# Another account for the split of the maxima, and order rules for seven attention steps

## The chip, the cores and the metric

The kernel runs on one core of a Trainium2 chip. The metric is the device time of one execution in microseconds. The core has a matrix engine (TensorE, PE in the profile), a vector engine (VectorE, DVE), a scalar engine (ScalarE, ACT), GpSimd (POOL) and a queue that issues transfers (SyncE, SP). They run side by side, each through its own list of instructions in order, and wait for each other by semaphores.

## The reference

A transformer block with a modulation by a condition, on 8 sequences of 1024 tokens with 512 features, 16 heads of 32, all in f32:

```python
mod = jax.nn.silu(condition) @ Wada + bada
sh_a, sc_a, gt_a, sh_m, sc_m, gt_m = jnp.split(mod, 6, axis=1)
xn = _layernorm(x, g1, be1)
xm = xn * (1.0 + sc_a[:, None, :]) + sh_a[:, None, :]
x = x + gt_a[:, None, :] * _attention(xm, Wqkv, Wproj, bproj)
xn = _layernorm(x, g2, be2)
xm = xn * (1.0 + sc_m[:, None, :]) + sh_m[:, None, :]
h = jax.nn.gelu(xm @ W1 + b1, approximate=False)
x = x + gt_m[:, None, :] * (h @ W2 + b2)
```

`_attention` is causal: scores of q and k times 32^-0.5, masked above the diagonal, softmax over the keys, times v, and the projection.

## The kernel before

The tokens are worked in 16 blocks of 512; blocks 2b and 2b+1 are the halves of sequence b. All linear layers (q, k, v, the projection, the two layers of the MLP) are products in the manner of Strassen: seven block products in place of eight, with sums of weights kept in DRAM and sums of activations (`t_a`, `t_m`, `qT`, `hT`) made on VectorE or GpSimd. Their matmuls (L233) go to three banks of PSUM and are taken out by ScalarE (L217) or VectorE (L222).

Attention goes through the groups (n, g): block n and four of the heads, g = 0 to 3. For a group, TensorE computes scores with the queries on the partitions (`sc`, L1828). VectorE adds the mask where the diagonal is (L1842) and reduces them to a maximum for each query and head (`mx`, L1845); in an odd block the two halves are combined (L1859). `split_maxima` writes each maximum as three bf16 numbers into `mcols` with four small instructions (L1864 to L1867), on GpSimd or VectorE. TensorE transposes them into a bank (L1883), ScalarE copies them out as `mrow` (L1889). Then TensorE computes the transposed logits less the maxima (`st`, L1909 and L1921), ScalarE takes the exponential (`pT`, L1934), GpSimd blanks the masked triangle (L1939) and adds the weights for the sums (L2047), and TensorE multiplies with v (`po`, L1962) and sums the weights (L1983). `sc` and `st` share one region of PSUM, called "st" in the code. So each must wait until the one before has been reduced or exponentiated.

Attention alone doesn't fill TensorE. The products of the linear layers are a second stream, cut in pieces of four matmuls, and the program is written down by a planner that runs as the kernel is built. It keeps an account of when each engine would be free (`now`) and each result there (`written`, `left`); every instruction that it emits adds a fixed number of ns by `note`. Before each step of attention, `step_aside` emits linear products until the account says that the step's operands are ready. Nothing of this account is seen by the chip: it decides only in which order the instructions stand on each engine, and, in `sooner` and `either`, which engine gets an elementwise instruction.

Two numbers of that planner can be set for each group (n, g), in the table `MANNER`; groups that don't stand in it have (1000, 0):

```python
margin[0], leaning[0] = MANNER.get((n, g), (1000, 0))
```

The first, `margin`, is the lead in ns that VectorE must have over GpSimd in the account for `either` to give it an instruction. The second, `leaning`, is by how many ns `step_aside` lets a step of attention go ahead of, or after, linear products: ahead of its operands' readiness when the linear stream is behind its due share, and otherwise as soon as its own wait is no longer than that of the linear stream by more than so much.

Blocks 3 to 13 have their normalised rows turned by transfers before the MLP: SP writes the rows to DRAM (`turned_m<-xm_m`, L852) and reads four columns back (`xm_m<-turned_m`, L858); VectorE or ScalarE modulates each column (L918, L924), and sums of them are made (L932, L934, L187, L190) for the products that read `xm_m` and `t_m`. Weights come through a ring of nine tiles (`w`, L391 and L393), loaded in order as a tile is released by its last product.

Of the kernel before, what the change touches and what calls it, by code (L numbers as in the profile page):

```python
# [22 lines left out]
def kernel(  # L23
# [81 lines left out]
    def due(reads=(), writes=()):  # L105
        t = 0.0
        for k in reads:
            t = max(t, written.get(k, 0.0))
        for k in writes:
            t = max(t, left.get(k, 0.0))  # L110
        return t

    def give_way(start, end):

        if not any(start <= a < end for a, *_ in pool_spans):
            return
        for i, (a, b, reads, writes) in enumerate(pool_spans):
            if a < start:
                continue
            if a >= end:  # L120
                break
            later = end, end + b - a
            pool_spans[i] = *later, reads, writes
            for of, keys in ((left, reads), (written, writes)):
                for k in keys:
                    if of.get(k) == b + SYNC:
                        of[k] = later[1] + SYNC
            end = later[1]
        now["POOL"] = max(now["POOL"], end)

    def note(engine, ns, reads=(), writes=(), port=False):
        start = max(now[engine], due(reads, writes))
        if port:
            start = max([start] + [b for a, b, *_ in pool_spans if a <= start < b])
            give_way(start, start + ns - FREE)
        elif engine == "POOL":
            start = max([start] + [b for a, b in port_spans if a <= start < b])
        end = start + ns
        now[engine] = end
        if port:  # L140
            port_spans.append((start, end - FREE))
            del port_spans[:-16]
        elif engine == "POOL":
            pool_spans.append((start, end, reads, writes))
            del pool_spans[:-16]
        for k in reads:
            left[k] = max(left.get(k, 0.0), end + SYNC)
        for k in writes:
            written[k] = end + SYNC
        return end  # L150
# [134 lines left out]
    for w in range(1, NB):  # L285
        n = w - 1
# [26 lines left out]
    n = NB - 1  # L313
# [145 lines left out]
    for some in row_sets:  # L459
        count = sum(n for _, n in some)  # L460
        rows = tmp.tile([P, TB], F32, tag="y", name=f"rows_{first_row}")[:count, :P]
# [1246 lines left out]


    TRIANGLE = [[0], [1, 3], [2]]  # L1710
    MANNER = {(0, 1): (1000, 300), (0, 3): (1000, 300), (1, 3): (-1000, 0), (2, 0): (-1000, 0), (2, 1): (2500, 0), (3, 1): (0, 0), (4, 0): (1000, 300), (6, 0): (1000, 300), (8, 0): (1000, 300), (10, 0): (1000, 300), (12, 1): (2500, 0), (14, 3): (0, 0), (3, 3): (2500, 300)}
    groups = [(n, g) for n in range(NB) for g in range(NC)]

    def score_units(n, g):
# [54 lines left out]
    def scores(n, g, parts):  # L1769

        h = blocks[n][1]
        for gg in {part[4]: None for part in parts}:
            if (n, gg) not in maxima:
                maxima[n, gg] = small.tile([P, 2, NTT, HPG], F32, tag="mx", name=f"mx_{n}_{gg}")
        reads = [("qT", n), ("kT", n - h + parts[0][1])]
        if (
            linear_wait() > 3000
            and not any(live)
            and wait_of((reads, ["st"])) > wait_of((reads, [BANK])) + 1000
        ):  # L1780
            scores_by_heads(n, g, parts, reads)
        else:
            scores_at_once(n, g, parts, reads)
        if units[unit_at[0] + 1 :] == [] or units[unit_at[0] + 1][:2] != (n, g):
            split_maxima(n, g, h)
# [64 lines left out]
    def split_maxima(n, g, h):  # L1850


        mx = maxima.pop((n, g))
        m = mx[:, 0, :, :]
        split = mcols.rearrange("p t (j c) -> p t j c", c=hd)
        high, middle, low = (split[:, :, :, i] for i in range(3))
        rest = small.tile([P, NTT, HPG], F32, tag="rest", name=f"rest_{n}_{g}")
        if h:
            nc.vector.tensor_tensor(m, m, mx[:, 1, :, :], ALU.max)  # L1859
            note("DVE", 180, [("mx", n, g)], [("mx", n, g)], port=True)  # L1860
        ready = due([("mx", n, g)])
        on_pool = max(now["POOL"], ready) + 1000 < max(now["DVE"], ready) + 2200
        engine = nc.gpsimd if on_pool else nc.vector
        engine.tensor_copy(high, m)  # L1864
        engine.tensor_tensor(rest, m, high, ALU.subtract)
        engine.tensor_copy(middle, rest)
        engine.tensor_tensor(low, rest, middle, ALU.subtract)  # L1867
        for _ in range(4):
            if on_pool:
                note("POOL", 250, [("mx", n, g)], [("rows", n, g)])  # L1870
            else:
                note("DVE", 180, [("mx", n, g)], [("rows", n, g)], port=True)
        rows_due.append((n, g))
# [176 lines left out]
    def attend():  # L2050
        previous = None
        for n in range(NB):
# [23 lines left out]
            for g, k, n_slots, upto in slots:  # L2076
                margin[0], leaning[0] = MANNER.get((n, g), (1000, 0))
                if (n, g) == groups[-1]:
# [153 lines left out]
```

## Time and profile before

| | |
|---|---|
| time, median of 3 runs | 3445.95 us |
| the runs | 3452.72, 3445.95, 3444.2 us |
| the profiled execution: its own time | 3444.65 us |
| its span, first to last instruction | 3442.9 us |
| TensorE, matmuls busy | 3414.4 us (99%) |
| VectorE busy | 2070.1 us (60%) |
| GpSimd busy | 1920.2 us (56%) |
| ScalarE busy | 1283.6 us (37%) |
| transfers, read and written over the span | 140 GB/s |
| granted TensorE clock | 1.000 |

Busy time is the time in which an instruction of the engine runs. TensorE's share leaves 28.5 us of the span; the other engines' idle time costs nothing as long as TensorE doesn't wait for them. A row of the waits names the waiting engine and line, what it waited for, and the total, the number and the longest of these waits in us. In rows of the timeline stand start, duration, engine, line, what is written and read, and in square brackets the idle time of the engine before it and what ended that.

### The profile page before, as it was taken

Reading aid. Unit: us, or ns where it says so; the run is one execution under the profiler, and the core shown is the slowest. Engines: PE = TensorE matmul, PEld = TensorE weight load, DVE = VectorE, ACT = ScalarE, POOL = GpSimd, SP = SyncE. Lnnn points to the kernel's source line nnn. Section 1 sums busy time; section 2 is a strip of 40 time slices with the busy share of each in tenths; the row PEclk is TensorE's granted clock in tenths of the full one; section 3 lists DMA queues with packets and bytes.
Section 4 is the critical chain, followed back from the end, with each engine's and each line's share of the span. In section 5 each row is a group of like instructions: output and inputs, shape, how many; then the busy total and the mean of one; then the engine's idle time right before and its main releaser. Section 6 shows DMA issues by size and latency. Waiting matters only on the chain.

```text
span 3442.9 us, 122860 instructions
## 1 busy us (share of the span) xinstructions
PE 3414.4 (99%) x55594; PEld 1772.7 (51%) x55594; DVE 2070.1 (60%) x2317; ACT 1283.6 (37%) x1418; POOL 1920.2 (56%) x2088
## 2 busy tenths in 40 slices
PE   8999999999999999999999999999999999999999
PEld 5544554455544555455554455454554545545555
DVE  6765666647566475664657546575566756556463
ACT  2345244333243333434344342432524335142431
POOL 3576755756267572675626755377553765447430
PEclk9999999999999999999999999999999999999999
DMA  6842434345544455444544445444464454533444
GB/s 231 279 129 85 119 116 137 102 120 156 170 136 130 129 159 157 133 139 130 167 142 133 136 137 171 136 133 141 129 186 129 126 149 148 167 109 103 121 142 137
DMA packets 380532, 490.69 MB, mean 143 GB/s; under 512 B 28487, under 2 KB 236511, under 8 KB 380010
## 3 DMA queue, kind: packets, MB, share of 16 engines
q1 hardware_dynamic: 379814, 482.54, 46.8%
q8 instruction: 438, 7.18, 0.9%
q14 instruction: 84, 0.69, 0.1%
q10 hardware_dynamic: 196, 0.28, 0.0%
HBM read 429.18 MB, written 53.53 MB: 140 GB/s over the span
## 4 chain that ended last, share of the span: by engine, by line
PE 92%; ACT 3%; DVE 3%; DMA 1%; issue 1%; POOL 1%; SPq 0%; DVEq 0%; ACTq 0%; POOLq 0%
PE bank L233 64%; PE sc L1828 9%; PE po L1962 7%; PE st L1921 7%; PE st L1909 3%; PE bank L1983 2%; DVE mx L1845 1%; ACT pT L1934 1%; ACT hT L1331 1%; PE bank L1883 0%; DMA xm_m<-turned_m 0%; DVE sc L1842 0%; ACT L1331 0%; PE bank L909 0%; ACT L170 0%
## 5 line engine op out<-in xcount | busy, mean ns | idle before, releaser
L2047 POOL TENSOR_TENSOR pT<-pT,pT 128x256 f32<-128x256 f32 (+3 forms) x1254 | 1221.5, 1010 | 173.9 <-ACT pT L1934 136.2
L1934 ACT ACTIVATE pT<-st 128x2048 f32<-128x2048 f32 x288 | 541.2, 1879 | 974.6 <-PE st L1921 884.0
L233 PE MATMUL bank<-w,hT 128*32 128x256 f32 x14336 | 812.9, 380 | 0.0
L1845 DVE TENSOR_REDUCE mx<-sc 128x4 f32<-128x2048 f32 (+3 forms) x384 | 665.6, 1754 | 210.5 <-PE sc L1828 204.3
L233 PEld LDWEIGHTS bank<-w,hT 128*32 128x32 f32 x14336 | 454.3, 110 | 357.0 <-issue 72.3
L233 PE MATMUL bank<-xm_m,w 128*32 128x256 f32 x8192 | 500.2, 380 | 0.8 <-ACT p_u L217 0.8
L233 PE MATMUL bank<-t_m,w 128*32 128x256 f32 x6144 | 381.2, 380 | 0.2
L233 PEld LDWEIGHTS bank<-xm_m,w 128*32 128x32 f32 x8192 | 255.0, 110 | 229.2 <-issue 65.4
L1939 POOL TENSOR_SCALAR_AFFINE_SELECT pT<-pT 128x512 f32<-128x512 f32 x256 | 172.2, 691 | 351.4 <-ACT pT L1934 349.9
L1828 PE MATMUL sc<-kT,qT 32*128 32x512 f32 (+3 forms) x3072 | 329.1, 520 | 1.3 <-DVE mx L1845 1.1
L1842 DVE TENSOR_TENSOR sc<-sc,mask 128x1024 f32<-128x1024 f32 (+1 forms) x160 | 162.8, 1017 | 245.3 <-PE sc L1828 181.5
L1962 PE MATMUL po<-pT,v 128*32 128x512 f32 (+3 forms) x3072 | 304.5, 491 | 0.0
L1921 PE MATMUL st<-qT,kT 32*128 32x512 f32 (+3 forms) x3072 | 300.0, 486 | 0.0
L233 PEld LDWEIGHTS bank<-t_m,w 128*32 128x32 f32 x6144 | 189.8, 110 | 174.7 <-issue 45.6
L233 PE MATMUL bank<-xm_a,w 128*32 128x256 f32 x3968 | 238.8, 380 | 1.7 <-ACT xm_a L924 1.1
L190 POOL TENSOR_TENSOR qT<-top,rec 128x512 f32<-128x512 f32 x58 | 75.4, 1300 | 284.2 <-ACT rec L2001 280.6
L1828 PEld LDWEIGHTS sc<-kT,qT 32*128 32x128 f32 x3072 | 129.4, 183 | 159.6 <-issue 59.2
L222 DVE TENSOR_TENSOR hT<-bank,u_u 128x512 f32<-128x512 f32 x192 | 129.5, 685 | 122.3 <-PE bank L233 119.4
L233 PE MATMUL bank<-w,qT 128*32 128x256 f32 (+1 forms) x3008 | 187.7, 389 | 0.0
L233 PE MATMUL bank<-t_a,w 128*32 128x256 f32 x2944 | 178.8, 380 | 0.5 <-DVE qT L222 0.5
L233 PEld LDWEIGHTS bank<-xm_a,w 128*32 128x32 f32 x3968 | 126.4, 110 | 100.6 <-issue 18.6
L1331 ACT ACTIVATE hT<-hT,cols 128x512 f32<-128x512 f32 x256 | 164.0, 711 | 17.8 <-DVE hT L222 17.1
(251 smaller groups left out, 3393.9 us busy)
## 6 DMA issues: line engine op xcount, KB each, us to landing
w<-in_L_cond_W_dram SPq DMA_DIRECT2D x384, 256.0 KB
w<-kept_up_S SPq DMA_DIRECT2D x256, 256.0 KB
w<-kept_down_S SPq DMA_DIRECT2D x256, 256.0 KB
w<-kept_qkv_S SPq DMA_DIRECT2D x180, 256.0 KB
w<-in_L_cond_Wqkv_dram SPq DMA_DIRECT2D x147, 256.0 KB
hat<-in_x_dram SPq DMA_DIRECT2D x64, 256.0 KB
xr<-in_x_dram SPq DMA_DIRECT2D x64, 256.0 KB
out_dram<-xr SPq DMA_DIRECT2D x64, 256.0 KB
```

The lines of the kernel that those rows point to most:

```text
L222: nc.vector.tensor_tensor(out, src, other, op)
L233: nc.tensor.matmul(ps[r], columns, rhs, start=start, stop=stop, skip_group_check=True)
L1331: nc.scalar.activation(hT[:, i, :], hT[:, i, :], AF.Gelu, bias=cols[:, O_B1 + f : O_B1 + f + 1])
L1828: nc.tensor.matmul(sc[:, j, c0 : c0 + w], qTs[n][r, gg, ts(qt, P)], keys_of(n, kh)[r, gg, :w], start=True, stop=True, skip_group_check=True,)
L1842: nc.vector.tensor_tensor(place, place, shape_of.to_broadcast(place.shape), ALU.add)
L1845: nc.vector.tensor_reduce(maxima[n, gg][:, kh, qt, :], sc[:, :, c0 : c0 + w], axis=AX.X, op=ALU.max)
L1909: nc.tensor.matmul(st[:, j, c0 : c0 + w], minus_ones[r, :], row[r, TB - w :], start=(c0 == 0), stop=False, skip_group_check=True,)
L1921: nc.tensor.matmul(st[:, j, c0 : c0 + w], kT[r, gg, ts(k % NTT, P)], qT[r, gg, TB - w :], start=False, stop=True, skip_group_check=True,)
L1934: nc.scalar.activation(pT[:, :, :used], st[:, :, :used], AF.Exp, scale=scale)
L1939: nc.gpsimd.affine_select(diagonal, diagonal, pattern=[[0, HPG], [1, P]], compare_op=ALU.is_ge, fill=0.0, base=0, channel_multiplier=-1,)
L1962: nc.tensor.matmul(po[r, TB - w :], v[:, k % NTT, g * P + j * hd : g * P + (j + 1) * hd], pT[:, j, c0 : c0 + w], start=(k == 0), stop=last ...
L2047: nc.gpsimd.tensor_tensor(into, into, pT[:, j, c0 : c0 + w], ALU.add)
```

## The change

One number of the account and seven entries of the table:

```diff
-    MANNER = {(0, 1): (1000, 300), (0, 3): (1000, 300), ..., (3, 3): (2500, 300)}
+    MANNER = {(0, 1): (1000, 300), (0, 3): (1000, 600), ..., (3, 3): (2500, 300), (10, 3): (-1000, 0), (0, 2): (2500, 300), (4, 2): (2500, 0), (2, 3): (0, 0), (6, 1): (1000, 300), (12, 2): (2500, 0)}
...
         for _ in range(4):
             if on_pool:
-                note("POOL", 250, [("mx", n, g)], [("rows", n, g)])
+                note("POOL", 335, [("mx", n, g)], [("rows", n, g)])
```

Four notes stand for the four instructions of a split on GpSimd, so the account of a split goes from 1000 to 1340 ns. The entry of (0, 3) goes from (1000, 300) to (1000, 600); six groups that had (1000, 0) get entries of their own. What is computed stays. The instructions on TensorE are the same in number and kind; elementwise instructions move between VectorE, ScalarE and GpSimd.

Three places show how the order moves. The names have block and group in them (`sc_9_0_1_0`: scores of block 9, group 0, query tile 1, key half 0; `xm_m7`: block 7's modulated input of the MLP); a last number counts buffers. The first place is TensorE at the transposition of the second group's maxima (block 0, group 1), the rows of before and then those of now:

```order
L1921 MATMUL st_0_0_1_958<-qT_0_399,kT_0_304 128x384 x4
L1921 MATMUL st_0_0_1_958<-qT_0_399,kT_0_304 128x128 x4
L1883 LDWEIGHTS mcols_162
L1883 MATMUL bank_2_97<-ident_b_170,mcols_162 32x128
...
L1962 MATMUL po_0_0_1003<-pT_0_0_0_868,v_0_640 32x512 x4
L233 MATMUL bank_1_96<-t_a1_608,w_16_604 32x256 x8
```

```order
L1921 MATMUL st_0_0_1_958<-qT_0_399,kT_0_304 128x384 x4
L1921 MATMUL st_0_0_1_958<-qT_0_399,kT_0_304 128x128 x4
L233 MATMUL bank_1_96<-t_a1_608,w_16_604 32x256 x8
L1883 LDWEIGHTS mcols_162
L1883 MATMUL bank_2_97<-ident_b_170,mcols_162 32x128
...
L1962 MATMUL po_0_0_1021<-pT_0_0_0_868,v_0_640 32x512 x4
```

Eight matmuls of a linear product that stood behind the transposition now stand ahead of it.

The second place is TensorE at the first scores of block 9, among the first products of block 7's MLP, before and now:

```order
L233 MATMUL bank_2_97<-t_a9_19618,w_657_20563 32x256 x16
L1828 MATMUL sc_9_0_0_0_20758<-kT_8_18068,qT_9_20462 128x512 x4
L233 MATMUL bank_0_95<-xm_m7_20155,w_658_20584 32x256 x16
L233 MATMUL bank_1_96<-t_m7_20156,w_660_20628 32x256 x8
L1828 MATMUL sc_9_0_1_0_20792<-kT_8_18068,qT_9_20462 128x512 x4
L233 MATMUL bank_1_96<-t_m7_20156,w_660_20628 32x256 x8
```

```order
L233 MATMUL bank_0_95<-t_a9_19618,w_657_20559 32x256 x16
L1828 MATMUL sc_9_0_0_0_20753<-kT_8_18110,qT_9_20460 128x512 x4
L233 MATMUL bank_2_97<-xm_m7_20155,w_658_20579 32x256 x16
L1828 MATMUL sc_9_0_1_0_20784<-kT_8_18110,qT_9_20460 128x512 x4
L233 MATMUL bank_1_96<-t_m7_20156,w_660_20624 32x256 x16
```

Between the first and the second group of scores stood 24 matmuls, and now stand 16.

The third place is the SP queue at the return of block 7's turned columns, before and now:

```order
L393 DMA w_653_20480<-kept_qkv_1_S2_271 128x512
L858 DMA xm_m7_20155<-turned_m7_20157 128x512 x2
L393 DMA w_654_20520<-kept_qkv_1_S1_268 128x512
L393 DMA w_655_20522<-kept_qkv_1_S3_286 128x512
L393 DMA w_656_20541<-kept_qkv_1_S4_289 128x512
L858 DMA xm_m7_20155<-turned_m7_20157 128x512
L391 DMA w_657_20563<-in_L0_cond_Wqkv_dram 128x2x256
L391 DMA w_658_20584<-in_L0_cond_W1_dram 128x2x256
L858 DMA xm_m7_20155<-turned_m7_20157 128x512
```

```order
L391 DMA w_657_20559<-in_L0_cond_Wqkv_dram 128x2x256
L1383 DMA out_0_dram<-xr_6_16528 4x32x512
L391 DMA w_658_20579<-in_L0_cond_W1_dram 128x2x256
L391 DMA w_659_20598<-in_L0_cond_W1_dram 128x2x256
L1383 DMA out_0_dram<-xr_6_16528 4x32x512 x2
L858 DMA xm_m7_20155<-turned_m7_20157 128x512 x4
L393 DMA w_660_20624<-kept_up_0_S2_1301 128x512
```

The four returns stood among the loads of w_653 to w_658 and now stand together behind w_659, after the stores of block 6. Block 9's columns move in the same way at block 11's first scores.

More of the change, by code (lines that the diff above doesn't have):

```diff
@@ L1710 @@
     TRIANGLE = [[0], [1, 3], [2]]
-    MANNER = {(0, 1): (1000, 300), (0, 3): (1000, 300), (1, 3): (-1000, 0), (2, 0): (-1000, 0), (2, 1): (2500, 0), (3, 1): (0, 0), (4, 0): (1000, 300), (6, 0): (1000, 300), (8, 0): (1000, 300), (10, 0): (1000, 300), (12, 1): (2500, 0), (14, 3): (0, 0), (3, 3): (2500, 300)}
+    MANNER = {(0, 1): (1000, 300), (0, 3): (1000, 600), (1, 3): (-1000, 0), (2, 0): (-1000, 0), (2, 1): (2500, 0), (3, 1): (0, 0), (4, 0): (1000, 300), (6, 0): (1000, 300), (8, 0): (1000, 300), (10, 0): (1000, 300), (12, 1): (2500, 0), (14, 3): (0, 0), (3, 3): (2500, 300), (10, 3): (-1000, 0), (0, 2): (2500, 300), (4, 2): (2500, 0), (2, 3): (0, 0), (6, 1): (1000, 300), (12, 2): (2500, 0)}
     groups = [(n, g) for n in range(NB) for g in range(NC)]
```

## The prediction

> **What bounds the kernel now.** I read the page's first lines, then a table of stretches, then the waits of TensorE between 62 and 3300 us, which is where the order of work can change: the orders of the two kernels are alike up to the second group of maxima, and again in the last 140 us.
>
> ```profile
> span 3442.9 us, 122860 instructions
> PE 3414.4 (99%) x55594; PEld 1772.7 (51%) x55594; DVE 2070.1 (60%) x2317; ACT 1283.6 (37%) x1418; POOL 1920.2 (56%) x2088
> ...
> 0.00:62.00 62.00, 49.94 (x787) 33.03 (x787) 36.05 (x62) 16.53 (x26) 23.27 (x34) 1.00 0.74 248
> 62.00:360.00 298.00, 291.30 (x4479) 144.09 (x4480) 198.95 (x216) 124.35 (x130) 195.78 (x221) 1.00 0.51 162
> 360.00:3300.00 2940.00, 2934.45 (x47928) 1516.45 (x47928) 1766.82 (x1943) 1119.20 (x1221) 1688.34 (x1828) 1.00 0.47 138
> 3300.00:3442.90 142.90, 138.68 (x2416) 79.10 (x2404) 68.29 (x99) 23.53 (x42) 12.80 (x6) 1.00 0.50 147
> ```
>
> TensorE is busy 99% of the span at the full granted clock (the 1.00 column). Its idle time is 298 - 291.30 = 6.70 us between 62 and 360 us and 2940 - 2934.45 = 5.55 us from there to 3300: 12.25 us together. No other order of the same products can win more than that. What TensorE waits for there:
>
> ```profile
> PE st L1909 <- DVE mx L1845: 5.1, 12, 1.4
> PE bank L1883 <- POOL mcols L1867: 3.2, 4, 1.6
> PE sc L1828 <- DVE mx L1845: 1.1, 2, 0.7
> PE bank L909 <- ACT xh_m L736: 0.9, 3, 0.4
> PE bank L233 <- ACT p_u L217: 0.8, 1, 0.8
> PE bank L233 <- DVE u_q L222: 0.6, 2, 0.3
> PE bank L233 <- DVE qT L222: 0.5, 2, 0.3
> PE st L1909 <- ACT pT L1934: 0.3, 1, 0.3
> ```
>
> Columns: us in total, times, longest. Two kinds lead. The region "st" in PSUM, shared by the scores and the softmax's logits, is wanted again before VectorE has reduced it or ScalarE has taken its exponential (5.1 + 1.1 + 0.3 = 6.5 us). And the transposition of the maxima (L1883) comes before their split on GpSimd is done (3.2 us).
>
> **The change part by part.**
>
> *Work.* TensorE issues the same products, and it goes from one array shape to another 1184 times instead of 1183 (counted in the two orders). One such change costs what these rows leave over:
>
> ```profile
> 1736.43 1.14 PE L1828 MATMUL sc<-kT,qT 32*128 32x512 f32 x8
> 1737.50 1.93 PE L233 MATMUL bank<-xm_m,w 128*32 128x256 f32 x32
> 1739.25 1.05 PE L233 MATMUL bank<-t_m,w 128*32 128x256 f32 x16
> 1740.22 1.14 PE L1828 MATMUL sc<-kT,qT 32*128 32x512 f32 x8
> ```
>
> 32 records take 1739.25 - 1737.50 = 1.75 us, 0.219 for four; 16 would take 0.87, and the next scores come after 0.97. A change of shape is 0.1 us: **+0.1 us**. (The trace has two records for each f32 matmul of the order.)
>
> *The longer account, 335 for 250.* It alters no instruction: in both orders the same 61 of 64 splits are on GpSimd. The chip's own price is in these rows (minimum/median/maximum):
>
> ```profile
> L1864 POOL CAST mcols<-mx x61: 252/255/1257, 60.7 to 3243.6; 128x16 bf16<-128x16 f32 x61
> L1865 POOL TENSOR_TENSOR rest<-mx,mcols x61: 228/230/1029, 61.0 to 3243.9; 128x16 f32<-128x16 f32 x61
> L1866 POOL CAST mcols<-rest x61: 252/257/1217, 61.3 to 3244.2; 128x16 bf16<-128x16 f32 x61
> L1867 POOL TENSOR_TENSOR mcols<-rest,mcols x61: 267/271/1068, 61.7 to 3244.6; 128x16 bf16<-128x16 f32 x61
> ```
>
> 255 + 230 + 257 + 271 = 1013 ns in the median, against 1000 in the account before and 1340 after. So what it does is to put the transposition four matmuls later in many steps (my count of products between the last scores of a group and its transposition rises by 0.43 us in 18 of 64 groups). That pays only where TensorE waited:
>
> ```profile
> 61.99 0.41 PE L1883 MATMUL bank<-ident_b,mcols 128*32 128x128 bf16 x16 [1.61 <-POOL mcols L1867]
> ...
> 77.53 0.41 PE L1883 MATMUL bank<-ident_b,mcols 128*32 128x128 bf16 x16 [0.64 <-POOL mcols L1867]
> ...
> 396.98 0.41 PE L1883 MATMUL bank<-ident_b,mcols 128*32 128x128 bf16 x16 [0.27 <-POOL mcols L1867]
> ...
> 2959.01 0.41 PE L1883 MATMUL bank<-ident_b,mcols 128*32 128x128 bf16 x16 [0.71 <-POOL mcols L1867]
> ```
>
> The first lies ahead of all changes and stays. At 77.53 eight matmuls (0.87 us) come between: 0.64 goes. At 396.98 the lead grows by 1.3 us: 0.27 goes. At 2959.01 it grows by 0.43: 0.71 becomes 0.28. Together **-1.3 us**; bounds 0 (if GpSimd is busier before the split) and -1.6 (all three).
>
> *The hand-overs of "st".* A whole group of scores holds it until VectorE has reduced it:
>
> ```profile
> 1737.63 2.29 DVE L1845 TENSOR_REDUCE mx<-sc 128x4 f32<-128x2048 f32 x1 [0.38 <-PE sc L1828]
> ...
> 962.47 2.28 DVE L1845 TENSOR_REDUCE mx<-sc 128x4 f32<-128x2048 f32 x1
> ...
> 964.81 0.40 PE L1909 MATMUL st<-mrow,minus_ones 32*128 32x512 bf16 x4 [0.15 <-DVE mx L1845]
> ```
>
> The reduction that belongs to the scores of 1736.43 ends at 1739.92, and TensorE starts 0.06 us after such an end (964.75 to 964.81). From the start of a group to the earliest next use are 3.49 + 0.06 = 3.55 us. TensorE fills this with the group itself (1737.50 - 1736.43 = 1.07 us), linear products and a change of shape. With 24 matmuls of products between: 1.07 + 2.63 + 0.1 = 3.8, no wait. With 20: 3.36, a wait of 0.19. With 16: 2.93, a wait of 0.62. Where the mask is added first, it is longer:
>
> ```profile
> 2178.04 1.14 PE L1828 MATMUL sc<-kT,qT 32*128 32x512 f32 x8
> ...
> 2179.30 0.70 DVE L1842 TENSOR_TENSOR sc<-sc,mask 128x512 f32<-128x512 f32 x1 [0.97 <-PE sc L1828]
> 2180.03 2.29 DVE L1845 TENSOR_REDUCE mx<-sc 128x4 f32<-128x2048 f32 x1
> ```
>
> 2182.32 - 2178.04 + 0.06 = 4.34 us; with 20 matmuls between it is short by 0.98. I went through all 575 hand-overs in both orders in this way. Before, those that are too short come to 6.2 us after 62 us, where the rows show 6.5, so the count can be trusted to some 5%. After, they come to 9.2 us, in 28 places instead of 15. The largest new ones: the scores of block 9 and of block 11 (first pair of each), 16 matmuls instead of 24, 0.62 us each; the masked scores of block 1's second group, 20 instead of 32, 0.98; smaller ones of 0.1 to 0.5 among block 0 and 1's steps. Two of 1.4 and 0.7 us in block 1 shrink to 0.6 and 0. The sum is **+3.0 us**. Bounds: -6.5 (all of it hidden) and +6 (twice the count, if in the moved steps VectorE comes to each reduction late by as much again).
>
> *What changes engine.* 26 elementwise instructions leave GpSimd and 35 come to it from VectorE; ScalarE takes eleven more of the modulated columns of blocks 7 to 13. VectorE is idle 40% and GpSimd 44% of the span, so I put it at nothing; the cover is that idle time. If it is gone, the price is a slower VectorE instruction while GpSimd works:
>
> ```profile
> L187 DVE TENSOR_TENSOR t_m<-xm_m,t_m x13: 691/692/1657, 219.7 to 3172.6; 128x512 f32<-128x512 f32 x13
> ...
> 1712.62 1.28 POOL L190 TENSOR_TENSOR y_d<-y_d,row_gm 128x512 f32<-128x512 f32 x1 [2.84 <-DVE y_d L222]
> ```
>
> The same subtraction takes 0.69 us as a rule and 1.66 at worst: up to 0.97 us for one that meets a GpSimd instruction. The Trainium skill, SBUF — State Buffer, section "SBUF: two separate sides", says that VectorE with two SBUF inputs and GpSimd hold one pair of ports in turn, each for its whole instruction. By that rule a meeting could cost the 1.28 us of the GpSimd row instead of 0.97; the row's worst case agrees in kind and is smaller, and the measurement is used.
>
> *Transfers.* The columns of blocks 7 and 9 come back from their turn through DRAM later: the last of the four returns is issued 6.4 us of TensorE's products ahead of the first that needs the columns, and was 14.6 us ahead. All four now stand in a row behind loads of weights and stores on the SP queue.
>
> ```profile
> 1714.01 1.62 SPq L858 DMA_DIRECT2D xm_m<-turned_m  x2
> ...
> 1721.28 0.55 DVE L918 TENSOR_SCALAR xm_m<-xm_m,gainm,shiftm 128x512 f32<-128x512 f32 x1 [1.77 <-DMA xm_m<-turned_m]
> ...
> 1724.89 2.19 SPq L1383 DMA_DIRECT2D out_dram<-xr  x3
> ...
> L924 ACT ACTIVATE xm_m<-xm_m,shiftm,gainm x15: 798/814/817, 882.1 to 2786.5; 128x512 f32<-128x512 f32 x15
> ```
>
> From issue to use took 1721.28 - 1714.01 = 7.27 us here, with VectorE waiting to the end. What holds the returns on the SP queue is not their row but the last load of weights ahead of them, which waits for a place in the ring; that place comes free 13.3 us of products before the first product of the columns. Two stores stand between (2.19 / 3 x 2 = 1.46 us); that product needs two columns: 1.62 us to issue both, 7.27 to land, 1.6 for two modulations. 1.46 + 1.62 + 7.27 + 1.6 = 12.0 us of 13.3. I take 0; the slack is 1.3 us at each of the two places, so the bounds are 0 and what the second rival below says.
>
> *Sum.* +0.1 - 1.3 + 3.0 = +1.8 us on the profiled execution of 3444.65 us (span 3442.9 and 1.75 around it): 3446.4. The median of the three runs, 3445.95, lies 1.3 above that execution; so **3447.7 us**. This is +0.05%, within the 0.3% (10.3 us) that a measurement of this kernel can tell from no change.
>
> **Rivals.**
>
> *Faster by over 0.3%.* The new steps hide waits that I don't follow, above all in blocks 0 and 1. For it: 6.70 us of the idle time lies between 62 and 360 us, where two of the seven rules act. Against: it needs 10.3 of all 12.25 us. Time if all of it went: 3445.95 - 12.25 = 3433.7. Chance 3%.
>
> *Slower: the returned columns land late.* Blocks 7 and 9 wait for the last column. For it: four returns at once behind a burst of loads. Against: the landing read above, 7.27 us, leaves 1.3. From 8.6 us on each further us of landing costs 2 us (two places); to pass 10.3 us over the median it needs (10.3 - 1.8) / 2 = 4.3 us more, a landing of 12.9. At 13.5 us: 3447.7 + 2 x 4.9 = 3457.5. Chance 4%.
>
> *Slower: GpSimd's added work holds up VectorE.* Each of the 35 instructions that come to GpSimd may stretch a VectorE one by 0.97 us, and that ahead of a reduction with no slack. Nine such meetings decide: 3447.7 + 9 x 0.97 = 3456.4. Against: most leave the hand-overs alone, since only 28 of 575 have no slack. Chance 5%.
>
> *It does nothing to the time for another reason*, for instance because the new short hand-overs are met by idle VectorE sooner than I count: 3445.95, inside the forecast's own case.
>
> **How the numbers follow.** The forecast's case, a sum of small waits within 0.3%, has 88%: the two slower cases 9%, the faster 3%. Its own range comes from the bounds of the terms (-1.6 and 0 for the splits, about -3 and +6 for the hand-overs) and the runs shown, which spread from 3444.2 to 3452.72: 3441 to 3454. The range that I give goes 1 us further down and to the first slower case: 3440 to 3457. Chances: faster 0.03, same 0.88, slower 0.09.
>
> **What would show it.** In the waits of TensorE after 62 us: "L1883 <- POOL mcols" falls from 3.2 to about 1.9 us, with nothing at 77 us; "st L1909" and "sc L1828 <- DVE mx" rise from 6.2 to about 9. At block 9's first scores the second group shows a wait of 0.6 us for the reduction. No wait of a product for "xm_m" or for a transfer at blocks 7 and 9. I am wrong if idle time of TensorE falls below 7 us or rises over 20 between 62 and 3300 us, or if another kind of wait than these two makes the difference.

## The result, and the profile after

The changed kernel takes 3456.9 us (median of 15 executions, 3450.36 to 3464.75); the kernel before, run beside it, 3445.84 us (15 executions, 3444.19 to 3452.72). The ratio is 1.0028, with a 95% interval of 1.0021 to 1.0036: slower by 9.7 us by this ratio, by 11.1 us by the two medians, at the edge of 0.3%. The forecast was +1.8 us.

The first lines of the page of the changed kernel, from an execution of 3456.08 us:

```profile
span 3454.4 us, 122840 instructions
PE 3418.0 (99%) x55594; PEld 1777.5 (51%) x55594; DVE 2078.9 (60%) x2310; ACT 1283.5 (37%) x1418; POOL 1939.2 (56%) x2097
```

The span is 11.5 us longer. TensorE is busy for 3.6 us more with the same matmuls, and idle for 7.9 us more. Where, the table of stretches tells. Columns: stretch, length, busy time of PE, PEld, DVE, ACT and POOL, then the granted clock of TensorE, the transfers' share and GB/s. The kernel before:

```profile
360.00:3310.00 2950.00, 2944.45 (x48112) 1522.43 (x48112) 1774.84 (x1952) 1119.75 (x1223) 1693.71 (x1830) 1.00 0.47 138
1700.00:1760.00 60.00, 59.67 (x1012) 32.26 (x1008) 31.45 (x35) 9.36 (x14) 14.18 (x11) 1.00 0.67 206
2150.00:2200.00 50.00, 50.00 (x816) 25.75 (x812) 30.50 (x30) 15.29 (x19) 7.42 (x12) 1.00 0.52 161
3100.00:3140.00 40.00, 40.00 (x604) 18.72 (x596) 27.56 (x30) 9.09 (x7) 31.95 (x33) 1.00 0.32 94
```

The changed kernel:

```profile
62.00:360.00 298.00, 291.62 (x4486) 144.06 (x4478) 204.84 (x220) 124.17 (x130) 194.42 (x217) 1.00 0.50 162
...
360.00:3310.00 2950.00, 2936.20 (x47883) 1520.18 (x47878) 1767.88 (x1929) 1117.48 (x1218) 1708.80 (x1841) 1.00 0.46 138
1700.00:1760.00 60.00, 56.93 (x937) 30.25 (x928) 26.50 (x29) 9.81 (x14) 13.51 (x10) 0.97 0.62 187
2150.00:2200.00 50.00, 46.58 (x756) 24.19 (x752) 29.61 (x30) 13.65 (x19) 2.42 (x2) 1.00 0.61 185
3100.00:3140.00 40.00, 35.34 (x508) 16.23 (x504) 25.84 (x21) 11.16 (x12) 24.43 (x26) 0.91 0.25 77
```

Nothing is lost up to 360 us. Three short stretches hold more idle time than is new in all, as some was won elsewhere: 2.7 us at 1700, 3.4 at 2150 and 4.7 at 3100. The first two are blocks 9 and 11, the third is block 14's projection, where the order is that of before. In the first and the third the granted clock is below 1.00 too. Shorter stretches show it at half, for 3.4 us from 1742.4 and for 6.8 us from 3114.55:

```profile
3114.60:3116.40 1.80, 0.00 (x0) 0.00 (x0) 1.80 (x2) 0.00 (x0) 0.65 (x1) 0.50 0.00 0
3116.50:3121.30 4.80, 4.80 (x36) 1.57 (x40) 2.37 (x2) 0.00 (x0) 0.00 (x0) 0.50 0.00 0
```

Of the 6.8 us the first 1.9 lie in a wait and cost nothing, so 4.9 us of matmuls run at half. Half of 3.4 and of 4.9 us are 1.7 and 2.5 us lost, which is about the 3.6 us that TensorE is busy for longer.

The waits of TensorE between 62 and 3310 us in the changed kernel (us in total, times, longest):

```profile
PE sc L1828 <- DVE mx L1845: 5.4, 6, 2.0
PE st L1909 <- DVE mx L1845: 5.0, 9, 1.2
PE bank L233 <- DVE p_proj L214: 4.7, 1, 4.7
PE bank L233 <- ACT xm_m L924: 2.3, 2, 1.3
PE st L1909 <- ACT pT L1934: 0.3, 1, 0.3
```

"L1883 <- POOL mcols" is gone from this stretch (its first wait, 1.61 us, now ends at 61.06). Two kinds are new: products that wait for modulated columns (`xm_m`, L924), and one product that waits 4.7 us for a copy on VectorE (`p_proj`, L214).

**The first two stretches.** Timeline of the changed kernel at block 9's first scores:

```profile
1723.62 2.46 SPq L1383 DMA_DIRECT2D out_dram<-xr  x2
...
1726.13 3.39 SPq L858 DMA_DIRECT2D xm_m<-turned_m  x4
...
1735.11 1.14 PE L1828 MATMUL sc<-kT,qT 32*128 32x512 f32 x8
...
1736.36 2.93 ACT L924 ACTIVATE xm_m<-xm_m,shiftm,gainm 128x512 f32<-128x512 f32 x4 [7.43 <-DMA xm_m<-turned_m]
...
1737.23 2.21 PE L233 MATMUL bank<-xm_m,w 128*32 128x256 f32 x32 [0.98 <-ACT xm_m L924]
...
1737.91 0.69 DVE L932 TENSOR_TENSOR xm_m<-xm_m 128x512 f32<-128x512 f32 x1 [3.70 <-DMA w<-kept_up_S]
...
1739.12 2.28 DVE L1845 TENSOR_REDUCE mx<-sc 128x4 f32<-128x2048 f32 x1
...
1741.46 1.23 PE L1828 MATMUL sc<-kT,qT 32*128 32x512 f32 x8 [2.03 <-DVE mx L1845]
```

The four returns are issued from 1726.13; the first modulation starts 10.23 us later. The product that reads the columns waits 0.98 us. More is lost behind it: in VectorE's row the difference of two columns (L932) and a sum for `kT` stand ahead of the reduction of the scores (L1845). The difference can't start before two columns are modulated, so the reduction starts at 1739.12, 4.0 us after the scores began, where it took 1.2 us before the change (1736.43 to 1737.63 in the rows of the prediction); and the second group of scores waits 2.03 us. (The row of L932 names a load of weights as what ended its wait; the second of the four modulations ended 0.03 us before it, at 1737.88, and at block 11 the same row names `xm_m` on ScalarE.) Block 11 repeats it with 1.3 and 2.02 us.

**The third stretch.** The same place in the kernel before and in the changed kernel, before first:

```profile
3101.42 6.00 POOL L2047 TENSOR_TENSOR pT<-pT,pT 128x384 f32<-128x384 f32 x8
...
3105.82 0.87 DVE L187 TENSOR_TENSOR qT<-t,qT 128x512 f32<-128x512 f32 x1 [4.16 <-POOL pT L2047]
3106.61 0.68 DVE L214 COPY p_proj<-bank 128x512 f32<-128x512 f32 x1
3107.34 0.64 PE L233 MATMUL bank<-w,qT 128*32 128x256 f32 x8
```

```profile
3105.79 5.56 POOL L2047 TENSOR_TENSOR pT<-pT,pT 128x384 f32<-128x384 f32 x8
...
3110.20 5.59 DVE L187 TENSOR_TENSOR qT<-t,qT 128x512 f32<-128x512 f32 x1 [4.16 <-PE bank L233]
3111.29 1.23 POOL L1939 TENSOR_SCALAR_AFFINE_SELECT pT<-pT 128x512 f32<-128x512 f32 x2
...
3112.48 2.77 POOL L2047 TENSOR_TENSOR pT<-pT,pT 128x256 f32<-128x256 f32 x4
...
3115.72 0.68 DVE L214 COPY p_proj<-bank 128x512 f32<-128x512 f32 x1
3116.46 1.08 PE L233 MATMUL bank<-w,qT 128*32 128x256 f32 x8 [4.66 <-DVE p_proj L214]
...
3117.47 2.09 PE L1828 MATMUL sc<-kT,qT 32*128 32x512 f32 x8
```

The subtraction on VectorE (L187, the third of the half sums for the projection's products) starts 4.40 us after GpSimd's row of eight additions in both, to a hundredth of a microsecond. It takes 0.87 us in the one and 5.59 in the other, where it ends only after GpSimd's last addition (3112.48 + 2.77 = 3115.25). The copy behind it holds a bank that TensorE needs. After the wait the same eight matmuls of scores take 2.09 us in place of 1.14. I call this the hold-up.

That it comes and goes by execution can be read from the times: the 15 executions of the changed kernel lie at 3450.36 to 3453.3 (five), 3455.76 to 3459.15 (nine) and 3464.75 (one).

### The profile page after: what moved, and what is told of

It reads as the page before. It is cut to its first block, busy times and chain, and to the rows that moved or that the text cites. A ratio compares the mean times of both kernels' runs of the same rounds, so it can differ in the third digit from the quotient of the medians.

```text
span 3454.4 us, 122840 instructions
## 1 busy us (share of the span) xinstructions
PE 3418.0 (99%) x55594; PEld 1777.5 (51%) x55594; DVE 2078.9 (60%) x2310; ACT 1283.5 (37%) x1418; POOL 1939.2 (56%) x2097
## 4 chain that ended last, share of the span: by engine, by line
PE 94%; DVE 3%; ACT 2%; DMA 1%; issue 0%; SPq 0%; POOL 0%; DVEq 0%; ACTq 0%
PE bank L233 65%; PE sc L1828 9%; PE po L1962 7%; PE st L1921 7%; PE st L1909 3%; DVE mx L1845 2%; PE bank L1983 2%; ACT pT L1934 1%; PE bank L1883 0%; DVE sc L1842 0%; ACT hT L1331 0%; DMA out_dram<-xr 0%; PE bank L909 0%; DMA xm_m<-turned_m 0%; DVE qT L187 0%
## 5 line engine op out<-in xcount | busy, mean ns | idle before, releaser
L1845 DVE TENSOR_REDUCE mx<-sc 128x4 f32<-128x2048 f32 (+3 forms) x384 | 665.5, 1754 | 160.2 <-PE sc L1828 153.9
L190 POOL TENSOR_TENSOR qT<-top,rec 128x512 f32<-128x512 f32 x52 | 67.0, 1288 | 252.1 <-ACT rec L2001 248.4
```

Of the source, the lines that this page charges most:

```text
L1845: nc.vector.tensor_reduce(maxima[n, gg][:, kh, qt, :], sc[:, :, c0 : c0 + w], axis=AX.X, op=ALU.max)
```

## The experiments

Two theories stood at the start: *late columns* (blocks 9 and 11, some 9 us) and *hold-up* (7 us at block 14, in some executions). Rival to both: the table of order rules costs time by itself. The first four kernels ran together on one chip, the next four on a second and the last four on a third, each time beside the kernel before. The changed kernel itself was not run again there, so its variants are compared with it only across chips. The kernel before turned out to have two levels of its own: of all its 102 executions, 70 were under 3449 us and 32 between 3449 and 3456.

**Each part alone.** First the account without the table (`e1_account`), then the table without the account (`e2_table`: the seven entries, with the account at 250).

```diff
-                note("POOL", 250, [("mx", n, g)], [("rows", n, g)])
+                note("POOL", 335, [("mx", n, g)], [("rows", n, g)])
```

> Only the account of the split goes from 250 to 335; the table stays that of before. The order then has the columns of blocks 7 and 9 coming back as late as in the changed kernel (the last return 6.4 us of products ahead of the first product). Theory 'late columns' (the two returns cost 5.0 and 3.8 us in the changed kernel): 3446 + 8.8 less some 3 us of gains among blocks 0 to 3 and at the splits, so 3450 to 3453, and 7 us more in executions in which a VectorE instruction at block 14's projection is held up by GpSimd. In the trace: the second score group of block 9 waits about 2 us for the reduction. Rival 'the table of order rules is the cause': 3444 to 3447, and no wait above 0.7 us at blocks 9 and 11.

> Only the seven entries of the table are changed; the account stays 250. The columns of blocks 7 and 9 come back as early as in the kernel before (14.6 us ahead). Theory 'late columns': no wait at blocks 9 and 11 above 0.3 us, time 3444 to 3449 (the counted short hand-overs are 9.7 us against 7.5 before, +2.2 at most), 7 us more where the hold-up at block 14 happens. Rival 'the table is the cause': 3452 to 3458.

Measured: the account alone 3471.01 us (6 executions, 3465.13 to 3479.55; ratio 1.0063, 1.0048 to 1.0078), the table alone 3465.77 us (8 executions, 3456.43 to 3469.1; ratio 1.0041, 1.0027 to 1.0055). Both medians are above that of the two together (its ratio is 1.0028, 1.0021 to 1.0036; the interval of the table alone reaches into that). They lie 11 and 10 us above what was expected even with one hold-up added (3460 and 3456). The waits of TensorE, account alone, then table alone:

```profile
PE sc L1828 <- DVE mx L1845: 9.3, 6, 2.3
PE bank L1983 <- POOL pT L2047: 3.7, 1, 3.7
PE bank L581 <- DMA b_gm<-in_L_cond_bada_dram: 2.9, 1, 2.9
...
PE bank L233 <- ACT xm_m L924: 1.8, 2, 1.4
```

```profile
PE bank L233 <- DVE p_proj L214: 9.4, 2, 4.7
PE st L1909 <- DVE mx L1845: 4.6, 9, 1.5
...
PE bank L581 <- DMA b_gm<-in_L_cond_bada_dram: 3.2, 1, 3.2
PE sc L1828 <- DVE mx L1845: 1.3, 4, 0.5
```

What each contributes is still seen. With the account alone the columns are late at four places (waits of 2.0 to 2.3 us for the reduction at 1329, 1756, 2183 and 2609 us); with the table alone at none, as theory had it, but there are two hold-ups, at 575 and 3123 us. The rest is new: with the account alone the sums of the weights wait for GpSimd's additions (L1983), and in both a product waits for a load at about 150 us (L581). So the parts don't add up: each order has its own short leads, and the table removes some that the account makes.

**The late return alone.** The kernel before, with the returns of blocks 7 and 9 put off.

```diff
-  transfers.append((queue_free[0] + LANDED, PATH, lambda c=c: get(c)))
+  transfers.append((queue_free[0] + (14000 if key in ("m7", "m9") else LANDED), PATH, lambda c=c: get(c)))
```

> The kernel before, with the return of the columns of blocks 7 and 9 put off by hand, so that the four returns stand in a row, 5.9 us of products ahead of the first product, and the two first score groups of block 9 have 16 matmuls between them, much as in the changed kernel. Theory 'late columns': both sites cost 3 to 5 us each, 3446 + 8 = 3454 (3451 to 3457), and 7 more where the hold-up at block 14 happens. Rival 'a late return is hidden, as the prediction had it': 0.6 us at each site from the short hand-over, 3447.

Measured: 3450.69 us (12 executions, 3446.95 to 3457.39) against 3449.64 for the kernel before (25), ratio 1.0008 (0.9999 to 1.0017). The profiled execution has 2.00 and 2.50 us of idle time at blocks 9 and 11 (stretches of 60 and 50 us with 58.00 and 47.50 busy), where the kernel before has 0.33 and 0. That is 4.2 us, between the theory and its rival. Its waits tell why: the products wait up to 1.0 us for `kT`, but no group of scores waits 2 us, since VectorE's row has the late instructions at another place, ahead of the sums for `kT`. So how late the columns are doesn't set the price alone; what stands behind the instruction that waits for them does.

**The hold-up.** One subtraction goes to GpSimd: at block 14 of the changed kernel (`e4_t3_gpsimd`), at block 14 of the kernel before (`e5_before_t3`), at blocks 2 and 14 of the changed kernel (`e6_after_t3_both`). The last argument is the lead that VectorE must have:

```diff
-  either(part[t], part[a], part[b], ALU.subtract, reads, [(key, t)])
+  either(part[t], part[a], part[b], ALU.subtract, reads, [(key, t)], NEVER if (n, t) == (14, "T3") else None)
```

For blocks 2 and 14 the condition reads `t == "T3" and n in (2, 14)`.

> The changed kernel, with one subtraction of block 14's projection (the third half sum) on GpSimd in place of VectorE; its first product comes 7 us after it. Theory 'hold-up' (in the profiled execution of the changed kernel this subtraction took 5.59 us in place of 0.7 on VectorE, and TensorE waited 4.66 us for the copy behind it and then ran at half rate): no execution has the wait, so the time is 3450 to 3452 and no longer spread over two levels. Rival 'the 7 us come from somewhere else, the long subtraction is only a sign': 3456 to 3458 as before this edit.

> The kernel before, with the third half sum of block 14's projection on GpSimd in place of VectorE, and nothing else. In the last runs the kernel before showed two levels, about 3445.5 and 3452, in 14 and 11 of 25 executions. Theory 'hold-up' (VectorE's subtraction there is let through at once, or only when GpSimd pauses 5 us later, and which of the two it is changes from one execution to the next): the upper level goes, all executions 3443 to 3448, so some 3 us faster in the median where the kernel before is in the upper level half of the time. Rival 'the levels come from another place': two levels as before, 3445 and 3452.

> The changed kernel, with the third half sum of the projections of blocks 2 and 14 on GpSimd. With block 14 alone it still had two levels, 3451 (5 executions) and 3458 (7). In the changed kernel's order the same subtraction stands at block 2 too, beside the eight additions on GpSimd (0.86 us, as at block 14 where it was let through). Theory 'hold-up, at block 2 as well': one level, 3449 to 3453. Rival 'the levels come from another place': two levels as before, 3451 and 3458.

Measured: `e4_t3_gpsimd` still has two levels, 3448.21 to 3452.53 (five executions) and 3457.36 to 3459.55 (seven), so block 14 isn't the only place. `e5_before_t3` has one, 3443.21 to 3447.38 (11), where the kernel before on that chip has 31 executions under 3449 and 4 at 3451.8 to 3454.53. With so few above, 11 of 11 below prove little by themselves. `e6_after_t3_both` has nine at 3447.16 to 3452.36 and three at 3458.52 to 3459.48: fewer, but not none. The profiled executions agree with the levels: 3456.08 us with one hold-up (the changed kernel), 3450.7 and 3449.55 with none (`e4_t3_gpsimd`, `e6_after_t3_both`).

The traces then showed what the places have in common. The eight additions of GpSimd are four long ones (1.0 us) and four short ones (0.46 us, 128x128). Block 2 before and after the change:

```profile
562.39 4.76 POOL L2047 TENSOR_TENSOR pT<-pT,pT 128x384 f32<-128x384 f32 x5
...
563.88 1.03 DVE L187 TENSOR_TENSOR qT<-t,qT 128x512 f32<-128x512 f32 x1 [0.60 <-PE bank L233]
```

```profile
562.24 4.07 POOL L2047 TENSOR_TENSOR pT<-pT,pT 128x384 f32<-128x384 f32 x6
...
564.71 0.86 DVE L187 TENSOR_TENSOR qT<-t,qT 128x512 f32<-128x512 f32 x1 [4.16 <-POOL pT L2047]
...
565.50 0.68 DVE L214 COPY p_proj<-bank 128x512 f32<-128x512 f32 x1
```

Before the change the subtraction comes 0.52 us into a long addition and is let in when that ends. After it, it comes 0.14 us into a short one, and the copy of `p_proj` is right behind it. The kernel before has one such meeting with a short addition (block 14), the changed kernel four (blocks 2, 8, 10 and 14). Over all 14 traces of this study the subtraction comes 0.06 to 0.21 us into a short addition 26 times: 20 times it is let in after it (0.8 to 0.95 us), six times it is held (5.6 to 6.7 us). In its 158 other meetings with GpSimd it was never held.

**Both causes away.** First the changed kernel with early columns (`e7_early_columns`: account 335 up to block 6, 250 from block 7), then the same with the subtractions of blocks 2 and 14 on GpSimd (`e8_early_columns_t3`).

```diff
-                note("POOL", 335, [("mx", n, g)], [("rows", n, g)])
+                note("POOL", 335 if n < 7 else 250, [("mx", n, g)], [("rows", n, g)])
```

> The changed kernel, with the account of a split at 335 for blocks 0 to 6 and at 250 from block 7 on. The order up to block 7 is that of the changed kernel; the columns of blocks 7 and 9 come back as early as in the kernel before. Theory 'late columns' (5.0 and 3.8 us at blocks 9 and 11): 8 us less than the changed kernel, so 3443 where no hold-up occurs and 3450 where one does. Rival 'e3 shows what they cost, some 2 us each': 3447 and 3454. Rival 'nothing': 3451 and 3458.

> The kernel of the run before this one (early columns) with the third half sums of blocks 2 and 14 on GpSimd: both causes taken away at once. If both theories hold: one level, 3442 to 3446, 0.1 to 0.2% faster than the kernel before, whose executions are spread over 3445 and 3452. If the hold-up theory falls: two levels, 3443 and 3450. If the late columns cost little: 3447.

Measured: `e7_early_columns` 3452.19 us (11 executions: one at 3444.75, five at 3448.51 to 3452.19, five at 3454.78 to 3461.95), with three meetings left. `e8_early_columns_t3` 3447.09 us (seven at 3444.28 to 3447.69, three at 3450.74 to 3451.35, one at 3456.89), with one meeting left, at block 10. The lowest level of the second has its median at 3446.2, that of `e6_after_t3_both`, with the late columns on the same chip, at 3449.6: 3.4 us less (5 us less than the lowest level of the changed kernel, 3451.5, on another chip), although a wait of 2.4 us has come at block 6's columns, where modulations and a difference stand ahead of a reduction. The expected single level wasn't there, because of block 10.

Then all meetings taken away: the subtraction on GpSimd at blocks 2, 8, 10 and 14 of the changed kernel (`e9_after_t3_all`), and the same at 2, 10 and 14 with the account 335 only up to block 4 (`e10_account5_t3`). In the edit of `e6_after_t3_both` the list then reads `(2, 8, 10, 14)` or `(2, 10, 14)`, in that of `e7_early_columns` the number is 5.

> The changed kernel, with the third half sum on GpSimd at all four blocks where the profile shows it beside GpSimd's short additions (2, 8, 10 and 14; the kernel before has one such block, 14). Theory 'hold-up': one level only, 3447 to 3452, with what the late columns cost (some 5 us over the kernel before) left in. Rival 'hold-ups come at other places too': two levels, 3450 and 3457.

> The changed kernel's table, the account of a split at 335 for blocks 0 to 4 and 250 from block 5 on (columns of blocks 7 and 9 early), and the third half sum of blocks 2, 10 and 14, which are the ones beside short additions here, on GpSimd. If late columns and hold-ups are all that the change costs: one level at 3442 to 3445. If the short hand-overs in blocks 0 and 1 cost what the prediction said (+3): 3446 to 3449.

Measured: `e9_after_t3_all` 3450.06 us, one level from 3447.96 to 3451.74 (11 executions). `e10_account5_t3` 3443.84 us, one level from 3441.62 to 3445.26 (11). The kernel before on that chip: 3447.37 (27 executions; 15 under 3449, 12 at 3449.65 to 3454.51). Ratios 1.0009 (1.0001 to 1.0018) and 0.9987 (0.9978 to 0.9995). On a chip where the kernel before has 12 of 27 executions above 3449, 22 executions of two kernels without such a meeting lie in one level each; with the held subtractions seen in the traces that settles the hold-up. And 3450.06 - 3443.84 = 6.2 us is what the changed kernel pays for its late columns, with all else in the blocks from 5 on that the account moves. The size is rough: the spans of the two profiled executions, 3447.3 and 3443.5 us, are 3.8 apart. Waits of `e9_after_t3_all`, then of `e10_account5_t3`:

```profile
PE sc L1828 <- DVE mx L1845: 5.4, 6, 2.0
PE st L1909 <- DVE mx L1845: 4.6, 8, 1.2
PE bank L233 <- ACT xm_m L924: 1.5, 2, 0.8
```

```profile
PE st L1909 <- DVE mx L1845: 6.8, 12, 1.3
PE bank L1883 <- POOL mcols L1867: 2.3, 2, 1.6
PE sc L1828 <- DVE mx L1845: 1.9, 5, 0.5
```

The wait for `p_proj` is gone from both; the waits for `xm_m` and the 2.0 us for the reduction are in the first alone. `e10_account5_t3` is faster than the kernel before by 0.13%, and by its ratio than the changed kernel too.

**Another account.** The table of before with the account at 290, and the subtraction of blocks 12 and 14 on GpSimd.

```diff
-                note("POOL", 250, [("mx", n, g)], [("rows", n, g)])
+                note("POOL", 290, [("mx", n, g)], [("rows", n, g)])
```

> The table of before with the account of a split at 290, and the third half sum of blocks 12 and 14 on GpSimd. The count of short hand-overs is 7.1 us (7.5 before), the columns of blocks 7 and 9 come early, those of block 11 in a row like blocks 7 and 9 of the changed kernel. With the late columns of one block: 3446 to 3449, one level. If that is hidden: 3443 to 3445, and then the fastest.

Measured: 3456.23 us (8 executions, one level, 3454.39 to 3459.14; ratio 1.0023, 1.0013 to 1.0032). One level was right, the time wrong by 7 us. Its trace has the late columns at block 13 (1.4 and 2.0 us at 2591 and 2595), but also the waits of `e1_account` that I hadn't counted: 3.7 us for the sums on GpSimd at 394, and 2.1 us for the load at 142. A count of the region "st" alone doesn't tell a good order from a bad one.

**What ends a hold-up.** The changed kernel with five more additions on GpSimd, into a spare tile, behind the row at the four places.

```diff
+        if (n, g) in ((3, 0), (9, 0), (11, 0), (15, 0)) and parts[0][2] == 2 * P:
+            spare = small.tile([P, 2 * P], F32, tag="spare", name=f"spare_{n}", bufs=1)
+            for _ in range(5):
+                nc.gpsimd.tensor_tensor(spare, acc[:, 0, TB - 2 * P :], acc[:, 1, TB - 2 * P :], ALU.add)
```

> The changed kernel, with five more additions on GpSimd (128x256, into a spare tile that nobody reads, 3.5 us together) right behind the row of additions and selections at the four places of the hold-up. GpSimd is idle there for 5 us otherwise. Theory 'VectorE gets in only when GpSimd pauses': executions without a hold-up stay at 3451, those with one go from 3458 to 3461 or 3462, those with two from 3465 to 3472; a held subtraction in the profile takes 9 us in place of 5.6. Rival 'it is held by something else, or for a fixed time': 3451, 3458 and 3465 as without the additions.

Measured: 3461.78 us (7 executions: two at 3450, one at 3457.9, four at 3461.78 to 3466.83). The profiled one has two hold-ups; the first:

```profile
565.49 6.30 DVE L187 TENSOR_TENSOR qT<-t,qT 128x512 f32<-128x512 f32 x1 [4.16 <-POOL pT L2047]
...
566.59 1.25 POOL L1939 TENSOR_SCALAR_AFFINE_SELECT pT<-pT 128x512 f32<-128x512 f32 x2
...
567.78 2.78 POOL L2047 TENSOR_TENSOR pT<-pT,pT 128x256 f32<-128x256 f32 x4
...
570.50 2.68 POOL L2052 TENSOR_TENSOR spare<-pT 128x256 f32<-128x256 f32 x3
```

It lasts 6.30 us, the other 6.74, neither 9 nor 5.6. Both end after the first of the five added ones (565.49 + 6.30 = 571.79; that addition starts at 570.50 and takes 0.74, as those of its size do). GpSimd's instructions overlap by a few hundredths, each of the four additions starting 0.68 us after the one before it and lasting 0.74; but the second added one starts 0.82 us after the first, whose tile it writes again. So in both VectorE got in at the first gap between two instructions of GpSimd, not at its pause, and a fixed time is ruled out (5.6, 6.30 and 6.74 us). The theory stands with "gap" for "pause"; my size was wrong.

## Why the prediction was right and wrong

The time lies 0.1 us inside the range, and "within 0.3%" holds by the median alone, as the interval reaches past 1.003. That is luck: the time is outside the range that the forecast's own terms gave (3441 to 3454), and the upper end that took it in, 3457, was set by a rival. The reasons were not the ones given: two of the conditions set for being wrong came true (20.2 us of idle time between 62 and 3310, and as much up to 3300, where 20 was the limit; and two other kinds of wait).

- *The longer account, -1.3 us.* Right in this term alone. The waits at 77, 397 and 2959 us are gone from the changed kernel, the one at the start remains: -1.6, the lower bound. The term leaves out what else the account moves: in the run with the account alone the columns are late at four places.
- *The hand-overs of "st", +3.0 us.* Mechanism right, size too large. The three rows come to 5.4 + 5.0 + 0.3 = 10.7 us where 9.2 was forecast, but 4.05 of them are the two waits behind late columns, for which the count had 1.24. The rest is 6.65 against 8.0 counted, and against 6.5 before: nothing lost.
- *Transfers, 0.* This step failed, by its own budget of 12.0 us of 13.3. The stores ahead of the returns took 2.46 us in place of 1.46; the last load of weights stood ahead of them for about 0.7 us (an estimate: by the budget's 13.3 us it could start at 1722.95, and the stores start at 1723.62), which the budget left out; from the first issue to the product it took 1737.23 - 1726.13 = 11.1 us where 10.5 was allowed. That is the 0.98 us of wait at the product. Worse, the budget ended at the product. The instruction of VectorE that reads the columns stood ahead of a reduction, and that wait, 2.0 us, is the larger. Two places, 3.0 and 3.4 us, and a slower clock after the first; 6.2 us between the medians of two kernels without a hold-up. The rival "columns land late", with a chance of 4%, had the wait for the columns but not the reduction behind it; every trace of this order shows both (the changed kernel and four of its variants).
- *What changes engine, 0.* This failed too. The prediction looked for the price in the 35 instructions that come to GpSimd. It was in an instruction that changes neither engine nor length: in three more blocks the subtraction on VectorE now asks just as a short addition starts. The rival "GpSimd holds up VectorE" put 0.97 us on a meeting and needed nine; one costs 4.7 us of wait and a slowed clock behind it, some 6.5 us between the levels, and one is what the median execution has, by its level. The row that gave 0.97 (13 instructions, 1.66 at worst) held no hold-up but a wait for the rest of one addition of 1.73 us. The Trainium skill, SBUF — State Buffer, section "SBUF: two separate sides", which was weighed there, has the loser blocked for one instruction of the other engine. The traces differ: 5.59 us, through the one under way and eight more.
- *The base.* The runs shown before were 3444.2, 3445.95 and 3452.72. The third was taken as scatter. By its size it was the upper of two levels, and so the one sign in the material that a hold-up may exist; no execution of the kernel before in that level was profiled.

So the changed kernel's 11 us of medians are about 6 for late columns, which every execution pays, and about 6.5 for a hold-up, which the median execution now meets once and did not meet before, less what was won elsewhere. The profiled execution adds up alike: 6.4 us of waits at blocks 9 and 11, 4.7 at block 14 and 4.2 by the slower clock are 15.3, of which 11.5 are left in the span.

## What to carry to other kernels

When a transfer moves in an order, follow the wait past its first reader: the instructions queued behind that reader on its engine, and who waits for them, can cost twice what the reader's own consumer does. Times in two separate levels can come from a race between engines, as here; look for an instruction on VectorE with two SBUF inputs beside an unbroken row of short GpSimd instructions, ahead of something that TensorE needs. Planner settings that were found together may not come apart: neither half of this change alone was faster than the whole.

## What the runs showed of the hardware that was not expected

An instruction of VectorE with two SBUF inputs can be passed over by a whole row of GpSimd instructions (the one under way and eight more, 5.6 us); in the two cases with a longer row it was let in at the first gap between two of them. It happened in 6 of 26 meetings 0.06 to 0.21 us into a 0.46 us addition and in none of 158 others; what decides between the two outcomes at the same offset (0.12 to 0.15 us in the held ones, 0.06 to 0.21 in the others) stays open.

A wait of a few microseconds can slow TensorE afterwards. After the wait of 4.66 us the granted clock is 0.50 until 4.9 us of matmuls have run, 2.5 us lost; after waits of 0.98 and 2.03 us with 2.2 us of products between it is 0.50 for 3.4 us, 1.7 us lost. At block 11 waits of 1.34 and 2.02 us left it at 1.00 in the same execution. One wait alone was followed by 3.4 us at 0.50 in `e1_account` (2.31 us, at 2609) and `e7_early_columns` (2.45 us, at 1531), and one of 2.44 us at the same place left it at 1.00 in `e8_early_columns_t3`. The Trainium skill, TensorE: Matmul & The Clock Gate, section "What's actually happening", gives half rate after an idle window of about 3.4 us that runs free of the kernel; by that 1.7 us would be lost per window, an estimate from that page. The half rate, the 3.4 us and two alike places that come out differently agree with it. That an idle time shorter than the window, 2.31 us here, can be enough is what the traces add.
